# The down projection of a pair as seven block products, with its banks released earlier

## The chip, the cores and the metric

The kernel runs on one core of a Trainium2 chip. The metric is device time in microseconds, from launch to end of the program on that core. Five engines take part: PE (matmul; its weight loads are shown as PEld), DVE (elementwise and reductions, reads SBUF and PSUM), ACT (activation functions and scaled copies), POOL (elementwise on SBUF, gathers by index) and SP (issues most transfers). Each runs its own instructions in order and waits for others at semaphores.

## The reference, cut to what matters

One transformer block on 4096 tokens of width 256, in f32. Both branches start from the normalised input `xn`.

```python
xn = layernorm(x)
# attention, 8 heads of 32, window of 64: each token sees 64 before and 64 after
o   = softmax(q k3 * scale, masked to the band) v3
x1  = layernorm2(xn + o @ Wo + bo)
att = x1 + gelu(x1 @ W1 + b1) @ W2 + b2
# experts: 8 of them, the 2 best per token, hidden width 816
h   = silu((xn @ gw[e].T + gb[e]) * (xn @ uw[e].T + ub[e]))
ffn = sum over the two experts of weight * (h @ down_w[e].T + down_b[e])
return x + att + ffn
```

The change concerns `h @ down_w.T + down_b`, the down projection of the experts.

## The kernel before, in words

**Stages.** A first stage (to about 79 us) normalises, projects keys, queries and values for the first groups, and computes the routing: each token goes to two slots, sorted by expert. Slots are cut into *units* of one expert each: a *pair* is two tiles of 128 tokens, a *single* is one tile. 34 units always run: 30 pairs and, as units 3, 7, 11 and 15, four singles. Five more run only if the routing needs them. After the units comes the second feed-forward stage of the attention branch (from about 861 us), which already uses seven block products in place of eight for its second matmul (`second`, line 1189).

**The loop over units** (line 1259). The engine order is written out by hand: the order of the calls is the order on every engine. Units 0 to 31 also carry a piece of attention: unit b treats query tiles i and i+1 (i even) and one half of the heads (hq = b % 2). A unit does, in this order:

- `gather(b+2)`: POOL fetches token rows for a later unit (L819).
- `scores`: PE (L960) into four banks; DVE adds the mask and takes the maximum, eight times 128x256 (L974). `apart`: POOL, two differences of values into `xd` (L1009).
- `down_rest` for unit b-1: PE, the last 48 hidden rows (L896). They lie twice in the chunk `FCM` of the hidden tile, at partitions 0 and 64, one for each tile of a pair.
- three gate/up chunks (`chunk`, i.e. `glu`: PE L845, ACT L853, DVE L854) are mixed with eight exponentials on ACT (L989) and four `merge`s on POOL: each adds the two halves of a head's keys (L1001) and then multiplies the second half with the identity matrix to keep its diagonal (L1002). Only chunks 0 and 1 come before the scaling.
- in even units `closing`: the output projection of two tiles finished earlier (PE L1074), its residual and statistics on DVE (L1077), and `residual`: a load and a POOL sum (L1067).
- `scale`: DVE takes reciprocals (L1019), multiplies the first halves (L1021, needs all merges' sums), sums the diagonals (L1022, needs the last L1002), L1023; POOL scales `xd` (L1025).
- `down` for unit b-1: PE `results` (L907), 6 chunks x 1 or 2 tiles; DVE adds the bias out of the banks (`summed`, L917); SP stores `y`; then the next down weights are loaded.
- `turned(b+1)`: PE transposes the next unit's rows (L832), DVE copies (L837). Units below 16 (and 16) also project keys, values or queries for a later group; units 3, 7, 11 and 15 queries, copied by DVE (L286).
- chunk 2, `flip` 0 (PE L1030, DVE two masked copies L1034), chunk 3, `flip` 1, `flip_rest` (PE transposes `xd`, L1043; ACT L1045), chunk 4, `glu_rest` (L862, L866, L869), silu on ACT (L886), chunk 5, `weigh` (PE L1052, reads the flips' copies), `outputs` (DVE L1061).

**What sets the order around the change.** Seven PSUM banks (pool `psm`) rotate through nearly all these steps: a tile takes the bank that was released first in the order of the calls. `xd` and the probabilities `pr` have one buffer each, down weights `wd` two, hidden tiles `hTs` two (units b-1 and b).

Of the kernel before, what the change touches and what calls it, by code (L numbers as in the profile page):

```python
# [55 lines left out]


REM = FE % P
REM_UP = P // 2
FM = FE - REM  # L60
FCM = FM // P
NT = S // P
G = 512
# [27 lines left out]
GU = BW + 2 * FCM + 1  # L91
DN = FCE * D + D
HQ = 4
# [8 lines left out]
def block_kernel(ctx: ExitStack, tc: tile.TileContext, a: dict, out: bass.AP):  # L102
# [118 lines left out]
    wqkv = pool(att, "wqkv", right)  # L221
    mask = wqkv.tile([P, 4, 2 * P], F32, tag="mask", name="mask")

# [87 lines left out]
    def make_mask():  # L311

        nc.gpsimd.memset(mask, 0.0)
        for kind in range(4):

            def keep(base, step, channel, m=mask[:, kind, :]):
                nc.gpsimd.affine_select(
                    out=m,  # L320
                    in_=m,
                    compare_op=ALU.is_ge,
                    fill=MASKED,
                    base=base,
                    pattern=[[step, 2 * P]],
                    channel_multiplier=channel,
                )

            keep(0, 1, -1)
            keep(2 * WIN, -1, 1)  # L330
            if kind == 0:
                keep(-WIN, 1, 0)
            if kind == 3:
                keep(2 * P - WIN - 1, -1, 0)
        for m, base, step in ((first_keys, 0, 1), (second_keys, -1, -1)):
            nc.gpsimd.memset(m, 1.0)
            nc.gpsimd.affine_select(
                out=m,
                in_=m,
                compare_op=ALU.is_ge,  # L340
                fill=0.0,
                base=base,
                pattern=[[-step, P]],
                channel_multiplier=step,
            )
# [542 lines left out]
    def silu_rest(hT):  # L888

        silu(hT, FCM, FCE, slice(0, REM_UP + REM if hT.shape[2] > P else REM))  # L890

    def results_rest(pds, w, hT):
        for t, pd in enumerate(pds):

            half = slice(t * REM_UP, (t + 1) * REM_UP) if len(pds) > 1 else slice(0, P)
            nc.tensor.matmul(  # L896
                pd,
                hT[half, FCM, t * P : (t + 1) * P],
                w[half, FCM * D : FCE * D],
                start=True,  # L900
                stop=False,
            )
# [11 lines left out]

    def summed(y, pds, w):
        for t, pd in enumerate(pds):
            nc.vector.tensor_tensor(y[:, t, :], pd, w[:, FCE * D :], ALU.add)  # L917

# [5 lines left out]

    def down(b, pds, w, hT):
        at, n, _ = UNITS[b]
        results(pds, w, hT)
        y = he.tile([P, TB, D], F32, tag="y", name=f"y{b}")[:, 0:n, :]
        summed(y, pds, w)
        nc.sync.dma_start(out=rows(done, at, n), in_=y)  # L930

    def whole(b, w, wd, xT, hT, banks, gss, y):

        _, n, _ = UNITS[b]
        n_in = n * P
        for k, f in enumerate([FCM] + list(range(FCM))):
            pb = halves(banks[k % 3])[:, :, 0:n_in]
            gs = gss[k % 3][:, 0:n_in]
            if f == FCM:
                rest_of(w, xT, hT, pb, gs)  # L940
            else:
                chunk_of(f, w, xT, hT, pb, gs)
            if f == FCM:
                silu_rest(hT)
            elif f % 2:
                silu(hT, f - 1, f + 1)
        pds = [banks[k][:, 0:D] for k in (3, 1)[:n]]
        results_rest(pds, wd, hT)
        results(pds, wd, hT)
        summed(y, pds, wd)  # L950

    def scores(i, hq):
# [3 lines left out]
        for j in range(2):  # L956
            lo = (i + j) % TG * P
            for hh in range(HQ):
# [7 lines left out]
                )  # L966
        kind = 0 if i == 0 else 2 if i == NT - 2 else 1
        pr = sp.tile([P, HQ, 2, 2 * P], F32, tag="pr", name=f"pr{i}_{hq}", bufs=1)
# [3 lines left out]
        for hh in range(HQ):  # L972
            for j in range(2):
                nc.vector.tensor_tensor_reduce(  # L974
                    out=pr[:, hh, j, :],
                    in0=ps[hh][:, j, :],
                    in1=mask[:, kind + j, :],
                    scale=-1.0,
                    scalar=-LOWEST,
                    op0=ALU.add,  # L980
                    op1=ALU.min,
                    accum_out=nm[:, j, hh : hh + 1],
                )
# [29 lines left out]

    def scale(i, hq, pr, sums, xd):

        rec = sp.tile([P, 2, HQ], F32, tag="rec", name=f"rec{i}_{hq}")
        same = sp.tile([P, 2, HQ], F32, tag="same", name=f"same{i}_{hq}")
        by_head = "p j h -> p h j"
        nc.vector.reciprocal(rec, sums)  # L1019
        first = pr[:, :, :, 0:P]  # L1020
        nc.vector.tensor_tensor(first, first, bcast(rec.rearrange(by_head), P, 3), ALU.mult)  # L1021
        nc.vector.tensor_reduce(same.rearrange(by_head), pr[:, :, :, P:], AX.X, ALU.add)  # L1022
        nc.vector.tensor_tensor(same, same, rec, ALU.mult)  # L1023
        xh = xd.rearrange("p j (h d) -> p j h d", h=HQ)
        nc.gpsimd.tensor_tensor(xh, xh, bcast(same, DH, 3), ALU.mult)  # L1025

    def flip(i, hq, j, pr):
# [3 lines left out]

        prT = [sp.tile([P, HQ, P], F32, tag="prT", name=f"prT{i}_{hq}_{j}"), pr[:, :, j, P:]]
        for t, m in zip(prT, (first_keys, second_keys)):
# [209 lines left out]
    for k in range(2):  # L1243
        nc.gpsimd.memset(hTs[k][:, FCM, :], 0.0)
    res = {0: residual(0)}
    xT = {}
# [12 lines left out]
    for b in range(ALWAYS):  # L1259
# [5 lines left out]
        def chunk(f):  # L1265
            glu(b, f, gus[b], xT[b], hT)

        if b + 2 < ALWAYS:
            xs[b + 2] = gather(b + 2)
        if attends:  # L1270
            pr, nm, sums = scores(i, hq)
            xd = apart(i, hq)
        if 0 < b < STEPS:
            pds = down_rest(b - 1, downs[b - 1], hTs[(b - 1) % 2])
        if b == 0:
            xT[0] = turned(0, xs.pop(0))
        if attends:
            exps(pr, nm, sums, 0, 3)
            merge(pr, 0)
        chunk(0)  # L1280
        if b >= STEPS:
            pds = down_rest(b - 1, downs[b - 1], hTs[(b - 1) % 2])
            down(b - 1, pds, downs.pop(b - 1), hTs[(b - 1) % 2])
        if attends:
# [7 lines left out]
        if hq == 0 and i - 2 in res:  # L1292
            closing(i - 2, oTs.pop(i - 2), res.pop(i - 2))
            if i < STEPS:
                res[i] = residual(i)
        if attends:
            scale(i, hq, pr, sums, xd)
        if b == STEPS:
# [16 lines left out]
        if b == STEPS + 1:  # L1315
# [4 lines left out]
            x2s[0] = second_loads(0)  # L1320
        if 0 < b < STEPS:
            down(b - 1, pds, downs.pop(b - 1), hTs[(b - 1) % 2])
        if b == ALWAYS - 1:
# [30 lines left out]
        if attends:  # L1354
# [4 lines left out]
            prT1 = flip(i, hq, 1, pr)  # L1359
            added = flip_rest(i, hq, xd)  # L1360
        if b:
            chunk(4)
        n = b - (ALWAYS - len(MAYBE))
        if n >= 0:
# [18 lines left out]
    pds = down_rest(ALWAYS - 1, downs[ALWAYS - 1], last)  # L1383
    down(ALWAYS - 1, pds, downs.pop(ALWAYS - 1), last)
    load_unit(ALWAYS + 2)
# [141 lines left out]
```

## Time and profile before

| what | us |
|---|---|
| three runs: median (lowest to highest) | 1088.48 (1086.47 to 1089.20) |
| the profiled execution, its own time | 1084.23 |
| its span, first to last instruction | 1082.1 |
| units with attention (0 to 31), from their first scores to the start of unit 32 | about 79 to 777 |

The profile page gives busy time by engine and by line. The groups that the change touches (line, engine, operation; busy in us, mean in ns):

| group | count | busy | mean |
|---|---|---|---|
| L907 PE, down projection, 128x256 | 768 | 171.6 | 379 |
| L896 PE, its last rows, 64x256 | 120 | 21.1 | 428 |
| L917 DVE, bias out of the bank, 128x256 | 64 | 24.6 | 418 |
| L1021 DVE, scaling, 128x1024 | 32 | 39.5 | 1236 |
| L1022 DVE, diagonal sums, 128x1024 | 32 | 39.1 | 1221 |
| L1034 DVE, masked copies of the flips, 128x512 | 128 | 87.0 | 680 |
| L1001 POOL, merges, 128x256 | 128 | 93.0 | 727 |
| L1002 POOL, diagonals, 128x256 | 128 | 125.2 | 978 |

A matmul's mean is longer than its spacing, since matmuls overlap in the pipeline: for PE the distance from start to start is what counts. In a timeline, each line has the start, the duration, engine, line and operation, output<-inputs, shapes, how many instructions were merged into it, and in brackets the idle time before it with what ended it.

### The profile page before, as it was taken

How to read it: one execution, taken by the hardware profiler on the slowest of the kernel's cores; microseconds unless marked ns; L12 is line 12 of the kernel's file. 1: busy time of each engine (PE TensorE's matmuls, PEld its weight loads, DVE VectorE, ACT ScalarE, POOL GpSimd, SP SyncE). 2: the span in 40 equal slices, each digit the busy share in tenths (PEclk: the TensorE clock that was granted, in tenths of full speed). 3: DMA queues.
4: the chain of work that ended last, by engine and by line, in shares of the span. 5: the costliest groups of instructions: out<-in, count | busy, mean ns of one | idle time of the engine just before them, and what ended most of it. 6: DMA issues, size and time to landing. Idle time of an engine off the chain costs nothing. (4 is left out here: it accounts for less than half of the span.)

```text
span 1082.1 us, 19049 instructions
## 1 busy us (share of the span) xinstructions
PE 1068.8 (99%) x6802; PEld 857.1 (79%) x6802; DVE 657.5 (61%) x1709; ACT 526.7 (49%) x1225; POOL 451.6 (42%) x599
## 2 busy tenths in 40 slices
PE   9998999999999999999999999999999999999998
PEld 6577887887888788888888888888788847777778
DVE  6665766657666566666666766666533355555546
ACT  4526456654556546746564566455424363333320
POOL 5516544455445444554455535544520043322220
PEclk9999999999999999999999999999999999999999
DMA  8252445544445354545444545445666443333121
GB/s 282 76 215 97 142 140 179 178 144 154 159 143 192 125 174 149 201 142 175 159 175 142 197 142 189 142 161 169 191 213 228 158 146 105 101 98 97 59 64 40
DMA packets 61040, 163.42 MB, mean 151 GB/s; under 512 B 6576, under 2 KB 46896, under 8 KB 51472
## 3 DMA queue, kind: packets, MB, share of 16 engines
q1 hardware_dynamic: 53632, 144.18, 38.2%
q0 software_dynamic: 6480, 17.70, 6.1%
q8 instruction: 55, 0.90, 0.3%
q10 hardware_dynamic: 832, 0.30, 0.1%
q14 instruction: 41, 0.34, 0.1%
HBM read 140.28 MB, written 21.89 MB: 150 GB/s over the span
## 5 line engine op out<-in xcount | busy, mean ns | idle before, releaser
L845 PE MATMUL gu<-xsT,wg 128*128 128x256 f32 (+1 forms) x1632 | 363.1, 369 | 1.6 <-issue 1.5
L845 PEld LDWEIGHTS gu<-xsT,wg 128*128 128x128 f32 x1632 | 289.0, 190 | 46.9 <-DVE nm L974 8.6
L853 ACT ACTIVATE gs<-gu,wg 128x256 f32<-128x256 f32 (+1 forms) x204 | 92.4, 453 | 257.8 <-PE gu L845 254.8
L854 DVE SCALAR_TENSOR_TENSOR hT<-gu,wg,gs 128x256 f32<-128x256 f32 (+1 forms) x204 | 95.0, 467 | 177.0 <-ACT gs L853 173.6
L1001 POOL TENSOR_TENSOR pr<-pr 128x256 f32<-128x256 f32 x128 | 93.0, 727 | 247.9 <-ACT pr L989 247.9
L907 PE MATMUL pe<-wd,hT 128*128 128x256 f32 x768 | 171.6, 379 | 0.0
L907 PEld LDWEIGHTS pe<-wd,hT 128*128 128x128 f32 x768 | 145.4, 190 | 20.5 <-issue 1.0
L1172 POOL DMA_INDIRECT got<-done,slot x64 | 64.5, 1008 | 176.6 <-DVE acc L1185 109.4
L1002 POOL TENSOR_TENSOR pr<-pr,ident 128x256 f32<-128x256 f32 x128 | 125.2, 978 | 10.0
L989 ACT ACTIVATE pr<-pr,nm 128x256 f32<-128x256 f32 x256 | 126.8, 497 | 0.4
L1127 PE MATMUL ph<-x2T,W 128*128 128x512 f32 x256 | 111.4, 593 | 1.1 <-ACT x2T L1117 1.1
L974 DVE CUSTOM_DVE_ANT_0 pr<-ps,mask 128x256 f32<-128x256 f32 x256 | 90.7, 420 | 19.3 <-PE ps L960 19.3
L1134 ACT ACTIVATE hf<-ph,b 128x512 f32<-128x512 f32 x64 | 43.4, 688 | 116.5 <-PE ph L1127 57.9
L886 ACT ACTIVATE hT<-hT 128x512 f32<-128x512 f32 (+3 forms) x148 | 80.9, 546 | 32.0 <-DVE hT L854 21.8
L1127 PEld LDWEIGHTS ph<-x2T,W 128*128 128x128 f32 x256 | 48.0, 190 | 58.9 <-issue 52.9
L819 POOL DMA_INDIRECT xs<-xnd,token x71 | 68.8, 969 | 49.2 <-DVE paired_tiles L786 31.9
L1021 DVE TENSOR_TENSOR pr<-pr,rec 128x1024 f32<-128x1024 f32 x32 | 39.5, 1236 | 27.8 <-POOL pr L1001 27.8
L1208 DVE TENSOR_TENSOR acc<-u,acc 128x256 f32<-128x256 f32 x32 | 12.9, 423 | 70.9 <-ACT u L1211 70.3
L989 ACT ACT_TABLE_LOAD x31 | 39.8, 1283 | 23.8 <-DVE nm L974 23.7
L1022 DVE TENSOR_REDUCE same<-pr 128x8 f32<-128x1024 f32 x32 | 39.1, 1221 | 19.2 <-POOL pr L1002 19.2
L989 ACT ACTIVATION_READ_ACCUMULATOR pr<-pr,nm 128x1 f32 x256 | 48.5, 189 | 0.0
L1198 PE MATMUL s<-V,hv 128*128 128x128 f32 x384 | 44.2, 275 | 0.0
(231 smaller groups left out, 1572.0 us busy)
## 6 DMA issues: line engine op xcount, KB each, us to landing
wg<-in_gate_up SPq DMA_DIRECT2D x37, 1670.5 KB, 7.0
wd<-in_down SPq DMA_DIRECT2D x37, 1024.0 KB
done<-y SPq DMA_DIRECT2D x30, 256.0 KB
x<-in_x SPq DMA_DIRECT2D x8, 512.0 KB, 5.9
xnd<-xn SPq DMA_DIRECT2D x8, 512.0 KB
res<-xnd SPq DMA_DIRECT2D x16, 256.0 KB
x1d<-res SPq DMA_DIRECT2D x16, 256.0 KB
x<-x1d SPq DMA_DIRECT2D x8, 512.0 KB
```

The costliest lines, as they stand in the source:

```text
L819: nc.gpsimd.indirect_dma_start(out=x[:, t, :], out_offset=None, in_=xnd, in_offset=bass.IndirectOffsetOnAxis(ap=token[:, i : i + 1], axis=0),)
L845: nc.tensor.matmul(pb[:, k, :], w[:, lo : lo + P], xT[:, c, :], start=(c == 0), stop=(c == DC - 1),)
L853: nc.scalar.activation(gs, pb[:, 0, :], AF.Identity, bias=w[:, gb : gb + 1])
L854: nc.vector.scalar_tensor_tensor(hT[:, f, :], pb[:, 1, :], w[:, ub : ub + 1], gs, ALU.add, ALU.mult)
L886: nc.scalar.activation(hT[on, lo:hi, :], hT[on, lo:hi, :], AF.Silu)
L907: nc.tensor.matmul(pd, hT[:, f, t * P : (t + 1) * P], w[:, f * D : (f + 1) * D], start=False, stop=(f == FCM - 1),)
L974: nc.vector.tensor_tensor_reduce(out=pr[:, hh, j, :], in0=ps[hh][:, j, :], in1=mask[:, kind + j, :], scale=-1.0, scalar=-LOWEST, op0=ALU.a ...
L989: nc.scalar.activation(pr[:, hh, j, :], pr[:, hh, j, :], AF.Exp, bias=nm[:, j, hh : hh + 1], scale=-1.0, accum_out=sums[:, j, hh : hh + 1],)
L1001: nc.gpsimd.tensor_tensor(first, first, second, ALU.add)
L1002: nc.gpsimd.tensor_tensor(second, second, bcast(ident, 2, 1), ALU.mult)
L1127: nc.tensor.matmul(ph, W1[:, c, f * P : (f + 1) * P], x2T[:, c, :], start=(c == 0), stop=(c == DC - 1),)
L1172: nc.gpsimd.indirect_dma_start(out=y, out_offset=None, in_=done, in_offset=bass.IndirectOffsetOnAxis(ap=slot[:, k, i : i + 1], axis=0),)
```

## The change

For a pair whose down projection falls into units 1 to 31, the six full chunks are no longer 2 tiles x 6 chunks of 128x256. The hidden tile and the weights are cut into 2 x 2 blocks (two token tiles, even and odd chunks, two halves of the output columns), and the Winograd form of Strassen's scheme makes the result from seven products of blocks with 3 chunks of 128x128 each. It needs sums of blocks beforehand and afterwards:

- `sums_of_down`: four subtractions of weights on POOL, 128x384 each, behind `apart`; one overwrites a block of the weights.
- `sums_of_experts_hidden`: three sums of hidden blocks on DVE behind the scores, ahead of chunk 0; a fourth (line 970) stands on DVE between the first product and the last.
- `results_of_pair`: the products; three go into the two banks of the unit, four share one further bank `sh`.
- `summed_of_pair`: ACT copies the shared bank into `y`; DVE adds within `y`, then adds the two banks.

PE does these products where `down` stood, ahead of `turned`. On DVE the sums behind them stand between the scaling and the diagonal's sum: `scale` is cut in two, and `scale_rest` comes after. `flip_rest` moves from before chunk 4 to after it. The bias of the down projection becomes a row of the weights behind the last 48 rows; the hidden tiles carry ones in rows 48 and 112, set once by POOL after the first gathers. The weights lose their broadcast bias (1024 to 896 KB), and `summed` becomes a copy. Silu on the last rows runs on 48 rows for each tile, so that the ones stay. The flips' first copy is written in place into `pr`, and the mask has three kinds in place of four; both free room.

```diff
-        silu(hT, FCM, FCE, slice(0, REM_UP + REM if hT.shape[2] > P else REM))
+        for t in range(hT.shape[2] // P):
+            silu(hT[:, :, t * P : (t + 1) * P], FCM, FCE, slice(t * REM_UP, t * REM_UP + REM))
...
+    def sums_of_down(b, w):
+        ts = he.tile([P, 3, FCH, P], F32, tag="ts", name=f"ts{b}", bufs=1)
+        t2, t3, t4 = (ts[:, k] for k in range(3))
+        m = blocks_of_weights(w)
+        b11, b12, b21, b22 = m[:, 0, 0], m[:, 0, 1], m[:, 1, 0], m[:, 1, 1]
+        t1 = b12
+        for out_, left_, right_ in ((t3, b22, b12), (t1, b12, b11), (t2, b22, t1), (t4, b21, t2)):
+            nc.gpsimd.tensor_tensor(out_, left_, right_, ALU.subtract)
+        return ts
+
+    def sums_of_experts_hidden(b, hT):
+        ss = he.tile([P, 2, FCH, P], F32, tag="ss", name=f"ss{b}", bufs=1)
...
+        nc.vector.tensor_tensor(s1, a21, a22, ALU.add)
+        nc.vector.tensor_tensor(s2, s1, a11, ALU.subtract)
+        nc.vector.tensor_tensor(a21, a11, a21, ALU.subtract)
+        return ss
+
+    def results_of_pair(b, pds, w, hT, ss, ts):
...
+        shared = bank(f"sh{b}").rearrange("p (k n) -> p k n", n=P)
+        product(pds[0][:, c1], n[:, 0, 1], m[:, 1, 0], stop=False)
+        nc.vector.tensor_tensor(n[:, 0, 1], n[:, 0, 1], ss[:, 1], ALU.subtract)
+        product(pds[1][:, c1], n[:, 1, 1], ts[:, 2])
+        product(shared[:, 0], n[:, 0, 0], m[:, 0, 0], True)
+        product(shared[:, 1], ss[:, 1], ts[:, 0], True)
+        product(shared[:, 2], n[:, 1, 0], ts[:, 1], True)
+        product(shared[:, 3], ss[:, 0], m[:, 0, 1], True)
+        product(pds[0][:, c2], n[:, 0, 1], m[:, 1, 1])
+        return shared
+
+    def summed_of_pair(y, pds, shared):
+        q = y.rearrange("p t (h n) -> p (t h) n", n=P)
+        nc.scalar.copy(q, shared)
+        yield
+        nc.vector.tensor_tensor(q[:, 1], q[:, 0], q[:, 1], ALU.add)
+        nc.vector.tensor_tensor(q[:, 2], q[:, 1], q[:, 2], ALU.add)
+        both = q.rearrange("p (t h) n -> p h t n", h=2)
+        nc.vector.tensor_tensor(both[:, 1], q[:, 1:3], bcast(q[:, 3], 2, 1), ALU.add)
         for t, pd in enumerate(pds):
-            nc.vector.tensor_tensor(y[:, t, :], pd, w[:, FCE * D :], ALU.add)
+            nc.vector.tensor_tensor(y[:, t, :], pd, y[:, t, :], ALU.add)
...
-        prT = [sp.tile([P, HQ, P], F32, tag="prT", name=f"prT{i}_{hq}_{j}"), pr[:, :, j, P:]]
+        prT = [pr[:, :, j, k * P : (k + 1) * P] for k in range(2)]
...
     for k in range(2):
         nc.gpsimd.memset(hTs[k][:, FCM, :], 0.0)
+        for behind in (REM, REM_UP + REM):
+            nc.gpsimd.tensor_tensor(
+                hTs[k][:, FCM, :],
+                hTs[k][:, FCM, :],
+                ident[:, behind : behind + 1].to_broadcast([P, B]),
+                ALU.add,
+            )
...
         if attends:
             pr, nm, sums = scores(i, hq)
             xd = apart(i, hq)
+        ts = ss = None
+        if 0 < b < STEPS and UNITS[b - 1][1] > 1:
+            ts = sums_of_down(b - 1, downs[b - 1])
...
             merge(pr, 0)
+        if ts:
+            ss = sums_of_experts_hidden(b - 1, before)
         chunk(0)
...
+        made = iter(())
+        if 0 < b < STEPS:
+            made = down(b - 1, pds, downs.pop(b - 1), before, (ss, ts))
+            next(made)
         if attends:
-            scale(i, hq, pr, sums, xd)
+            rec = scale(i, hq, pr, sums)
+            list(made)
+            scale_rest(i, hq, pr, rec, xd)
...
-        if 0 < b < STEPS:
-            down(b - 1, pds, downs.pop(b - 1), hTs[(b - 1) % 2])
...
             prT1 = flip(i, hq, 1, pr)
-            added = flip_rest(i, hq, xd)
         if b:
             chunk(4)
+        if attends:
+            added = flip_rest(i, hq, xd)
```

## The prediction

> **What bounds the kernel now.** I read the busy shares, then the chain that ended last, then the timelines of PE, DVE and POOL in single units. Busy shares:
>
> ```profile
> PE 1068.8 (99%) x6802; PEld 857.1 (79%) x6802; DVE 657.5 (61%) x1709; ACT 526.7 (49%) x1225; POOL 451.6 (42%) x599
> ```
>
> PE streams all the time, and its listed waits add up to some 10 us. So time falls only if PE gets less work, and rises by whatever makes PE wait. For PE's pace, PE's timeline in unit 3, and one piece of the chain of waits (start, duration, what):
>
> ```profile
> 149.50 5.35 PE L907 MATMUL pe<-wd,hT 128*128 128x256 f32 x24
> 154.69 0.60 PE L832 MATMUL pts<-ident,xs 128*128 128x128 f32 x4
> ```
>
> ```profile
> 891.64 12.51 PE s L1198 x112
> ```
>
> Start to start, 24 matmul records of 256 columns take 154.69 - 149.50 = 5.19 us, 0.216 each. The second stage already runs block products of 128 columns: 12.51 / 112 = 0.112 each. (A product of f32 tiles shows as two records.)
>
> Behind PE the other engines have uneven slack. The reader should look at unit 3 (one tile after a pair), DVE and PE:
>
> ```profile
> 155.27 1.22 DVE L1021 TENSOR_TENSOR pr<-pr,rec 128x1024 f32<-128x1024 f32 x1 [1.62 <-POOL pr L1001]
> 157.12 1.22 DVE L1022 TENSOR_REDUCE same<-pr 128x8 f32<-128x1024 f32 x1 [0.62 <-POOL pr L1002]
> 158.37 0.17 DVE L1023 TENSOR_TENSOR same<-same,rec 128x8 f32<-128x8 f32 x1
> 158.48 0.76 DVE L917 TENSOR_TENSOR y<-pe,wd 128x256 f32<-128x256 f32 x2
> 159.15 0.68 DVE L837 COPY xsT<-pts 128x512 f32<-128x512 f32 x1
> 159.75 1.40 DVE L286 TENSOR_SCALAR qt<-q,bq 128x512 f32<-128x512 f32 x2
> ...
> 163.38 0.68 DVE L1034 TENSOR_TENSOR pr<-pT,second_keys 128x512 f32<-128x512 f32 x1
> ...
> 164.22 0.40 PE L1052 MATMUL po<-prT,vt 128*32 128x128 f32 x8
> ```
>
> From L1022 on DVE has no gap, and its last masked copy ends at 163.38 + 0.68 = 164.06; PE reads it at 164.22. **Margin 0.16 us**: here DVE is as late as PE. Units 7, 11 and 15 show the same (252.82 against 252.99, 341.59 against 341.75, 430.35 against 430.51). The chain starts on POOL: the scaling L1021 waits for the fourth merge (L1001).
>
> **The change part by part.**
>
> *PE.* Units 1 to 31 without 4, 8, 12, 16 (whose predecessor is one tile) do the down projection of a pair: 27. Each had 24 records, 5.19 us; now 7 products x 3 chunks x 2 records = 42 at 0.112 = 4.69. Gain 0.50 each. Here a rule speaks against the change: the Trainium skill (TensorE: Matmul & The Clock Gate, Back-to-back issue gap) says that spacing in a stream of loads and matmuls is set by both, sustained 81 ns at N=128 against 131 at N=512. By that flat curve (linear between, 256 columns would be near 98) halving the columns would save 17%: 42 x 0.179 = 7.5 us, a loss of 2.3 per pair, 63 in all. But the trace has the very shape, f32 with a fresh load for each, at 0.112; I take the row. Upper bound by the 16 narrow records of unit 3 from 147.62 to 149.50: 0.1175 each, gain 0.25.
>
> *DVE before the scaling.* Three sums of 128x384, placed behind the scores and ahead of the first gate product, and a fourth inside the products. No row has 384; between 128x256 (0.42, L1208) and 128x1024 (1.22, L1159) it is 0.56. DVE's own gaps there (0.83 and 1.37 us in unit 3) hide three; the fourth needs DVE while PE runs five products of 0.67, so PE rarely waits for it (in unit 3, at worst 0.6, inside time that DVE sets anyway). What they do to POOL is not hidden. Two moments:
>
> ```profile
> 155.32 1.76 POOL L1002 TENSOR_TENSOR pr<-pr,ident 128x256 f32<-128x256 f32 x1
> ```
>
> ```profile
> 131.46 1.58 DVE L1021 TENSOR_TENSOR pr<-pr,rec 128x1024 f32<-128x1024 f32 x1 [0.47 <-POOL pr L1001]
> 131.23 0.73 POOL L1002 TENSOR_TENSOR pr<-pr,ident 128x256 f32<-128x256 f32 x1
> ```
>
> A POOL sum (0.73 alone) that starts under DVE's scaling takes 1.76: 1.03 lost to a DVE op of 1.22. In the one case where POOL was first, POOL kept 0.73 and DVE took 1.58 instead of 1.22. The Trainium skill (SBUF — State Buffer, Who interferes with whom) has it as a lock: a DVE instruction with two SBUF inputs shares a read interface with GpSimd, and whoever is first holds it for the whole instruction. The whole instruction would be 4 x 0.56 = 2.2 us on the merges; by the row (op less 0.19) it is 4 x 0.37 = 1.5. The merges run back to back from 150.04, just as the scores end, so there is no gap to take it. Least: 0.4, if most sums fall between POOL's instructions. I take 1.5.
>
> *DVE behind the scaling.* `summed_of_pair` adds two sums of 128x128 and one of 128x256, each dependent on the last: 0.29 (between 0.17 at 8 elements and 0.42) twice, 0.42, 0.1 between them: 1.1 us. The two adds out of the banks cost what L917 costs, only earlier. The 0.62 that L1022 waited for POOL's last merge goes into it; that merge now meets these sums: 0 to 0.5, say 0.25. The flips no longer write a tile of their own, same cost.
>
> *The chain in units 3, 7, 11, 15:* 1.5 + 1.1 - 0.62 + 0.25 = 2.2, less the margin 0.16: **2.1 us each, 8.4 in all** (0.7 to 2.6). There DVE sets the end, so PE's 0.50 does not show: 23 x 0.50 = 11.6 is left.
>
> *Odd units 17 to 31* (8, without projections for later groups):
>
> ```profile
> 678.31 1.23 DVE L1021 TENSOR_TENSOR pr<-pr,rec 128x1024 f32<-128x1024 f32 x1 [1.41 <-POOL pr L1001]
> 681.55 0.60 PE L1030 MATMUL pT<-ident,pr 128*128 128x128 f32 x4
> ```
>
> The flips need the scaling, done at 679.54: slack 2.0. PE comes 0.5 earlier, the scaling 1.5 later: none is left. Lateness carried from the even unit before then stalls PE one to one. If DVE has caught up (even units have 1.7 us more PE work, `closing`): 0. If POOL's residual sum (L1067, 1.27) gets in between the new DVE sums of an even unit: up to 1.6. I take 0.75 each, 6.0. Odd units below 16 with a pair have 1.7 us or more of projections on PE: nothing.
>
> *Start.* Four POOL sums of 128x256 put ones behind the hidden rows: 4 x 0.7 (0.73 in L1001, 0.62 in L1025) = 2.8, behind the first gathers and ahead of everything of unit 0:
>
> ```profile
> 84.42 0.46 POOL L1009 TENSOR_TENSOR xd<-vt 128x128 f32<-128x128 f32 x1
> 85.45 0.73 POOL L1001 TENSOR_TENSOR pr<-pr 128x256 f32<-128x256 f32 x1 [0.56 <-ACT pr L989]
> 92.53 0.65 PE L1030 MATMUL pT<-ident,pr 128*128 128x128 f32 x4 [0.48 <-DVE pr L1021]
> ```
>
> POOL waits here 0.56 and, at the second head, 0.53; the rest, 1.7, goes into the merges and on to the flips, for which PE waits already. 1.7 (1.2 to 2.2).
>
> *At nothing.* POOL's sums of down weights, 4 x 1.0 (between 0.73 at 256 and 1.27 at 512 elements), stand behind `apart` and two gathers; POOL idles 8.38 us before the first merge (L1001 in units 3, 7, 11, 15; similar elsewhere), of which the later scaling takes some 2.2: 2 us stay. With that gone they would delay merges, scaling and flips one to one. Their weights land a unit earlier, and with 896 instead of 1024 KB. ACT: the bank copy 0.59 in its gap of 5.15 us before the third gate product; two small silu instead of one, +0.2. Bias as a matmul row instead of an add: L917 becomes a copy out of PSUM, 0.42 either way. The transposes of `xd` go behind the fifth gate chunk, so L1009 starts 2 us later, in the same idle time. Banks: the order of instructions gives those of the down projection to the second flip and later; both are free by then. SP's queue keeps its order; the store of y comes earlier.
>
> **Sum:** -11.6 + 8.4 + 6.0 + 1.7 = +4.5 us. The profiled execution's own time is 1084.23 (span 1082.1), below all three runs shown; changed runs are measured like those, so I set the sum on their median: 1088.5 + 4.5 = **1093.0**.
>
> **The rivals.**
> *Port costs little* (faster): the chain takes 0.4 for the four sums and nothing for the last merge, so 0.4 + 1.1 - 0.62 - 0.16 = 0.7 in four units, odd units stall 0, start 1.2: -11.6 + 2.9 + 1.2 = -7.5, 1081. For it: DVE has 39% free and its gaps cover the sums. Against: both rows of the port above.
> *Balance* (no change): chain 2.0, odd units 0.25: -11.6 + 8.0 + 2.0 + 1.7 = +0.1, 1088.6. Decided by whether even units let DVE catch up.
> *POOL gets in everywhere:* 2.6 in four units, 1.6 in eight, start 2.2: -11.6 + 10.4 + 12.8 + 2.2 = +13.8, 1102.
> *Narrow products don't keep their pace* (the change doesn't do what it says): gain 0.25, 5.8 in all: +10.3, 1098.8. Against: 112 records at 0.112.
>
> **How the numbers follow.** Forecast 0.36, port costs little 0.28, balance 0.18, POOL everywhere 0.12, pace lost 0.06. This kernel's runs tell about 0.3% from no change, 3.3 us. Faster 0.28, same 0.18, slower 0.54. The range takes in the faster rival and most of the worst: 1080 to 1101; the forecast's own is 1090 to 1097.
>
> **What would show it.** Right: the block products at 4.7 us a pair; the scaling 1.5 us later behind the scores; POOL merges of 1.1 us under DVE's sums; in units 3, 7, 11, 15 PE waiting at `weigh` for DVE some 2 us; PE waits at the flips in odd units from 17. Wrong: merges still at 0.73 and no PE waits at `weigh` (faster), or waits inside the products for the fourth sum.

## The result and the profile after

| | median | lowest to highest | runs |
|---|---|---|---|
| before | 1086.83 us | 1086.44 to 1089.20 | 5 |
| after | 1081.93 us | 1081.21 to 1083.35 | 5 |

The ratio of after to before is 0.9951, with a 95% interval of 0.9938 to 0.9964: the change makes the kernel 0.5% **faster**. I had forecast 1093.0 us, slower. The kernel before was run again beside the experiments below, 35 runs in three groups with medians of 1087.44, 1087.12 and 1087.75.

The busy shares of the profiled execution of the changed kernel (1082.42 us, span 1080.7):

```profile
PE 1063.6 (98%) x7288; PEld 861.0 (80%) x7288; DVE 779.3 (72%) x1898; ACT 547.8 (51%) x1283; POOL 588.0 (54%) x709
```

DVE is busy 122 us longer and POOL 136 us, PE 5 us less. The kernel got faster all the same, because most of the new work lies in time that DVE and POOL had free. The table shows where it does not. A unit's length is the distance from the start of its first scores on PE's timeline to that of the next unit's:

| units | before | after | difference, us |
|---|---|---|---|
| 0 | 19.81 | 21.40 | +1.59 |
| 1, 2, 5, 6, 9, 10, 13, 14 and 17 to 31: pair behind a pair (23) | 20.85 to 24.09 | 20.36 to 23.61 | -0.49 each |
| 3, 7, 11, 15: single behind a pair | 18.86 | 20.43 | +1.57 each |
| 4, 8, 12 (pair behind a single) | 23.23 | 23.42 | +0.19 each |
| 16 (pair behind a single) | 20.69 | 20.88 | +0.19 |

From the first scores to the start of unit 31 (the length of unit 31 itself can't be read this way) these sum to 1.6 - 22 x 0.49 + 4 x 1.57 + 4 x 0.19 = -2.1 us; the traces show 676.39 before and 674.30 after. From there to the end this one execution took 326.89 us against 326.29 before, and six of the kernels below, with nearly the same work there, 325.8 to 326.4: the 0.6 us are not read as an effect of the change.

**The gain** is read in unit 23, PE's timeline after the change (start, duration, line):

```profile
589.21 0.83 PE L960 MATMUL pe<-wd,hT 128*128 128x128 f32 x6
589.88 0.83 PE L960 MATMUL pe<-ts,hT 128*128 128x128 f32 x6
...
593.90 0.60 PE L834 MATMUL pts<-ident,xs 128*128 128x128 f32 x4
594.33 1.89 PE L847 MATMUL gu<-xsT,wg 128*128 128x256 f32 x8
596.06 0.60 PE L1118 MATMUL pT<-ident,pr 128*128 128x128 f32 x4
```

Seven products take 593.90 - 589.21 = 4.69 us, 0.67 each and without a wait between them; and the flip (L1118) follows its neighbour without a bracket, so PE doesn't wait there for the scaling. In the kernel before, DVE's scaling and PE's flip of this unit stood so:

```profile
591.44 1.22 DVE L1021 TENSOR_TENSOR pr<-pr,rec 128x1024 f32<-128x1024 f32 x1 [1.41 <-POOL pr L1001]
594.67 0.60 PE L1030 MATMUL pT<-ident,pr 128*128 128x128 f32 x4
```

The scaling was done 2.0 us before the flip; after the change (L1100 below) 596.06 - 595.57 = 0.5 us are left.

**The cost** on DVE and POOL in the same unit; the sums of the hidden layer are L946, L947, L948 and L970, the merges L1082 and L1083:

```profile
587.87 0.55 DVE L946 TENSOR_TENSOR ss<-hT 128x384 f32<-128x384 f32 x1
588.46 0.97 DVE L947 TENSOR_TENSOR ss<-ss,hT 128x384 f32<-128x384 f32 x1
589.35 1.08 DVE L948 TENSOR_TENSOR hT<-hT 128x384 f32<-128x384 f32 x1
...
591.13 1.10 DVE L970 TENSOR_TENSOR hT<-hT,ss 128x384 f32<-128x384 f32 x1
...
594.34 1.23 DVE L1100 TENSOR_TENSOR pr<-pr,rec 128x1024 f32<-128x1024 f32 x1 [2.00 <-POOL pr L1082]
595.49 0.82 DVE L983 TENSOR_TENSOR y<-y 128x128 f32<-128x128 f32 x1
596.34 0.29 DVE L984 TENSOR_TENSOR y<-y 128x128 f32<-128x128 f32 x1
```

```profile
588.08 0.93 POOL L1082 TENSOR_TENSOR pr<-pr 128x256 f32<-128x256 f32 x1 [1.43 <-ACT pr L1070]
589.09 0.92 POOL L1083 TENSOR_TENSOR pr<-pr,ident 128x256 f32<-128x256 f32 x1
589.97 1.04 POOL L1082 TENSOR_TENSOR pr<-pr 128x256 f32<-128x256 f32 x1
...
593.58 0.73 POOL L1082 TENSOR_TENSOR pr<-pr 128x256 f32<-128x256 f32 x1
594.39 1.77 POOL L1083 TENSOR_TENSOR pr<-pr,ident 128x256 f32<-128x256 f32 x1
```

Alone a sum takes 0.55 and a merge 0.73. Where they overlap, both become longer, in turns: a merge waits for the sum that runs (0.93), the next sum for the merge (0.97), and so on. The sums lose more by it (0.4 to 0.55 each) than the merges (0.2 to 0.3). So the scaling L1100 starts 10.4 us after the first scores, against 9.4 before, 1.0 later. Behind it the last diagonal (L1083, 1.77) and the first sum of the results (L983, 0.82 instead of 0.29) meet in the same way.

**Where it can't be hidden**: unit 3, DVE, and then PE.

```profile
160.39 1.21 DVE L1108 TENSOR_REDUCE same<-pr 128x8 f32<-128x1024 f32 x1
...
161.72 0.68 DVE L839 COPY xsT<-pts 128x512 f32<-128x512 f32 x1
162.32 1.40 DVE L288 TENSOR_SCALAR qt<-q,bq 128x512 f32<-128x512 f32 x2
...
165.94 0.68 DVE L1122 TENSOR_TENSOR pr<-pT,second_keys 128x512 f32<-128x512 f32 x1
```

```profile
162.45 1.16 PE L847 MATMUL gu<-xsT,wg 128*128 128x128 f32 x8 [0.51 <-DVE xsT L839]
...
166.68 0.43 PE L1140 MATMUL po<-pr,vt 128*32 128x128 f32 x8 [0.17 <-DVE pr L1122]
```

DVE works without a gap from the scaling to the last masked copy, which ends at 165.94 + 0.68 = 166.62, and PE's last group of `weigh` starts just behind it. PE waits twice for this chain, and the unit is 1.57 us longer.

### The profile page after: what moved, and what is told of

The parts are those of the page before. It is cut to its first block, busy times and chain, and to the rows that moved or that the text cites. A ratio compares the mean times of both kernels' runs of the same rounds, so it can differ in the third digit from the quotient of the medians.

```text
span 1080.7 us, 20405 instructions
## 1 busy us (share of the span) xinstructions
PE 1063.6 (98%) x7288; PEld 861.0 (80%) x7288; DVE 779.3 (72%) x1898; ACT 547.8 (51%) x1283; POOL 588.0 (54%) x709
## 5 line engine op out<-in xcount | busy, mean ns | idle before, releaser
L1082 POOL TENSOR_TENSOR pr<-pr 128x256 f32<-128x256 f32 x128 | 114.1, 891 | 73.0 <-ACT pr L1070 73.0
L856 DVE SCALAR_TENSOR_TENSOR hT<-gu,wg,gs 128x256 f32<-128x256 f32 (+1 forms) x204 | 91.6, 460 | 65.7 <-ACT gs L855 64.3
L1083 POOL TENSOR_TENSOR pr<-pr,ident 128x256 f32<-128x256 f32 x128 | 132.5, 1035 | 10.0
L888 ACT ACTIVATE hT<-hT 128x512 f32<-128x512 f32 (+2 forms) x179 | 85.8, 486 | 49.6 <-DVE hT L856 25.2
L1055 DVE CUSTOM_DVE_ANT_0 pr<-ps,mask 128x256 f32<-128x256 f32 x256 | 90.7, 420 | 10.4 <-PE ps L1041 10.3
L1100 DVE TENSOR_TENSOR pr<-pr,rec 128x1024 f32<-128x1024 f32 x32 | 39.2, 1225 | 42.3 <-POOL pr L1082 42.3
L1113 POOL TENSOR_TENSOR xd<-xd,same 128x256 f32<-128x256 f32 x32 | 19.7, 615 | 84.7 <-DVE same L1111 84.6
L937 POOL TENSOR_TENSOR ts<-wd 128x384 f32<-128x384 f32 x54 | 54.1, 1002 | 2.1
L981 ACT COPY y<-sh 128x512 f32<-128x512 f32 x27 | 15.8, 585 | 58.9 <-PE sh L960 58.9
L960 PE MATMUL pe<-wd,hT 128*128 128x128 f32 x324 | 44.9, 275 | 0.0
```

The costliest lines, as they stand in the source:

```text
L856: nc.vector.scalar_tensor_tensor(hT[:, f, :], pb[:, 1, :], w[:, ub : ub + 1], gs, ALU.add, ALU.mult)
L888: nc.scalar.activation(hT[on, lo:hi, :], hT[on, lo:hi, :], AF.Silu)
L1055: nc.vector.tensor_tensor_reduce(out=pr[:, hh, j, :], in0=ps[hh][:, j, :], in1=mask[:, kinds[j], :], scale=-1.0, scalar=-LOWEST, op0=ALU.a ...
L1082: nc.gpsimd.tensor_tensor(first, first, second, ALU.add)
L1083: nc.gpsimd.tensor_tensor(second, second, bcast(ident, 2, 1), ALU.mult)
```

## The experiments

Each starts from the changed kernel and makes one edit, where nothing else is said. Times are to be compared with its 1081.93 us; ratios are to the kernel before. "Theory 1" and "theory 2" are those of the expectation just above.

### The block products are left out

```diff
-        if 0 < b < STEPS and UNITS[b - 1][1] > 1:
+        if 0 < b < 1 and UNITS[b - 1][1] > 1:
             ts = sums_of_down(b - 1, downs[b - 1])
```

> All pairs' down products are computed in full, nothing else is changed (the bias as a row of the rest, the later small transposes, the masked copies in place and the sums behind scaling stay). Theory 1: the block products are what the time came from, 0.49 us in each of 23 pair units less 1.77 us around each of four single units: without them 1081.9 + 11.3 - 7.1 = about 1086.1 us (ratio 0.9995 to the kernel before), with the first unit still 1.6 us longer and units 17 to 31 at 20.85 us. Theory 2: the shorter units come from the small edits (bias row, smaller weights' load, later transposes): 1075 to 1082 us (0.989 to 0.995).

Measured: 1088.58 us, ratio 1.0016 (1.0007 to 1.0025). The units are as theory 1 had it: 20.86 us in the odd ones from 17 (+0.49), 18.86 in units 3, 7, 11 and 15, the first still 21.39; 4, 8, 12 and 16 stay at 23.42 and 20.88. By its units the products are worth 23 x 0.49 - 4 x 1.57 = 5.0 us; the medians lie 6.65 apart, and where the rest comes from the traces don't show. The remaining edits alone make the kernel no faster, rather 1 us slower by the medians, and 2.3 by the units (1.58 in the first, 0.19 in each of four). The gain comes from the products.

### No block products in the four single units

```diff
-        if 0 < b < STEPS and UNITS[b - 1][1] > 1:
+        if 0 < b < STEPS and UNITS[b - 1][1] > 1 and UNITS[b][1] > 1:
```

> The block products are kept where the unit over them attends to a pair itself; in units 3, 7, 11 and 15 (a single block over a pair's down products) the pair's down is computed in full as before. Theory 1: in these four units the chain of VectorE (scaling, sums of the products, diagonal, queries, masked copies) sets the end, and the port lost 1.57 us in each and 0.20 us in the unit after it: units 3, 7, 11, 15 go back from 20.43 to 18.86 us between their scores, and the kernel to 1081.9 - 4 x 1.77 = about 1075 us (ratio to the kernel before 0.989). Theory 2: TensorE sets the end there too, and the four units lose the 0.49 us that the block products save: about 1084 us (0.997).

Measured: 1075.81 us, ratio 0.9893 (0.9879 to 0.9908). Units 3, 7, 11 and 15 take 18.87 us, and PE waits nowhere in them. Theory 1 holds for these four: there the chain of DVE takes more than the products give. Its other half falls: units 4, 8, 12 and 16 keep their 23.42 and 20.88, so their 0.19 us is not lateness carried over from the single unit.

### Without the sums of the hidden layer

```diff
-        nc.vector.tensor_tensor(s1, a21, a22, ALU.add)
-        nc.vector.tensor_tensor(s2, s1, a11, ALU.subtract)
-        nc.vector.tensor_tensor(a21, a11, a21, ALU.subtract)
-        return ss
+        return ss0
...
-        nc.vector.tensor_tensor(n[:, 0, 1], n[:, 0, 1], ss[:, 1], ALU.subtract)
```

> VectorE's four sums of the hidden layer are left out (the block products read a tile of zeros for the two sums and the two blocks unchanged), so the results of pairs in the attention units are not the reference's; all products and the sums behind them stay. Theory 1: these sums, taking turns with GpSimd's merges, cost the single units 0.9 us ahead of scaling and 0.5 us at the first sum behind it: merges at 0.73 us, scaling 8.3 instead of 9.2 to 9.3 us after the scores, units 3, 7, 11, 15 at 18.9 to 19.1 instead of 20.43 us, the kernel at 1081.9 - 4 x 1.4 - 4 x 0.2 = about 1075.5 us (0.989). Theory 2: what lengthens these units is the five sums behind the scaling, not the ones ahead of it: units 3, 7, 11, 15 stay above 20 us, and the kernel at about 1081 (0.9945).

Measured: 1078.56 us, ratio 0.9918 (0.9905 to 0.9931). Units 3, 7, 11 and 15 take 19.55 us, between the two theories: of the 1.57 us, 0.88 came from the sums ahead of the scaling. POOL and DVE in unit 3 of this kernel, whose line numbers are 8 lower in these places:

```profile
151.96 0.73 POOL L1074 TENSOR_TENSOR pr<-pr 128x256 f32<-128x256 f32 x1 [2.46 <-ACT pr L1062]
...
157.24 1.76 POOL L1075 TENSOR_TENSOR pr<-pr,ident 128x256 f32<-128x256 f32 x1
```

```profile
157.20 1.22 DVE L1092 TENSOR_TENSOR pr<-pr,rec 128x1024 f32<-128x1024 f32 x1 [1.62 <-POOL pr L1074]
158.34 0.81 DVE L975 TENSOR_TENSOR y<-y 128x128 f32<-128x128 f32 x1
```

The merges are back at 0.73, so it was the sums that had stretched them. But the first sum behind the scaling (L975) still takes 0.81: it meets POOL's last diagonal whenever that one starts together with the scaling, and costs 0.52 whether or not there were sums before. My theory 1 had put that down to the lateness.

### The queries evacuated by ACT in the four single units

```diff
-                    queries(ahead, c, False)
+                    queries(ahead, c, UNITS[b][1] < 2)
```

> In units 3, 7, 11 and 15 the two evacuations of the queries (0.67 us each) move from VectorE to ScalarE, nothing else. Theory 1: in these four units one gapless chain on VectorE, from the scaling to the second masked copy, sets the end; it becomes 1.3 us shorter, so the units go from 20.43 to about 19.1 us and the kernel to 1081.9 - 4 x 1.3 = about 1076.7 us (ratio 0.990). Theory 2: the wait is for GpSimd's merges or for a bank: the units stay at 20.4 us and the kernel at 1082 (0.995).

Measured: 1077.38 us, ratio 0.9913 (0.9896 to 0.9929); the four units take 19.13 us, 1.30 less. PE in unit 3 of this kernel:

```profile
164.40 0.88 PE L1140 MATMUL po<-pr,vt 128*32 128x128 f32 x24
165.45 0.43 PE L1140 MATMUL po<-pr,vt 128*32 128x128 f32 x8 [0.17 <-DVE pr L1122]
```

Work of 1.3 us taken off DVE shortens the unit by 1.3 us: DVE sets the end, and even now the last masked copy is what PE waits for. Theory 1 holds.

### The small transposes go back

```diff
             prT1 = flip(i, hq, 1, pr)
+            added = flip_rest(i, hq, xd)
         if b:
             chunk(4)
-        if attends:
-            added = flip_rest(i, hq, xd)
```

> Only the small transposes go back ahead of the fifth chunk, where they were before the change. Theory 1: that they come 1.7 us later is what keeps units 17 to 31 free of a stall: the small values are scaled 1.3 us after TensorE gets to them, so each of the eight odd units 17 to 31 becomes 1.3 us longer (20.37 to about 21.6 us) and the kernel about 1081.9 + 8 x 1.3 = 1092 us (ratio 1.004); the units with keys or values between are unchanged. Theory 2: the move is free either way, TensorE waits nowhere else more: 1082 us (0.995).

Measured: 1097.31 us, ratio 1.0096 (1.0080 to 1.0111). Theory 1 holds with its mechanism, and the place is larger than it said. PE in unit 23 of this kernel:

```profile
605.82 0.60 PE L1118 MATMUL pT<-ident,pr 128*128 128x128 f32 x4
607.62 0.44 PE L1131 MATMUL pX<-ident,xd 128*128 128x128 f32 x2 [1.20 <-POOL xd L1113]
```

The odd units 17 to 29 take 1.41 us more and the even ones 18 to 28 another 0.62 to 0.75, 13.8 us to the start of unit 31. The sums that DVE now does ahead of the diagonal's make the scaled `xd` late, and only the later place of its transposes hides it.

In this profile the first unit is 1.5 us longer as well, but the edit leaves that unit's order as it was. PE's clock fell there. The two flips of the first unit in this kernel, a row of its stretches (us, each engine's busy time, PEclk the granted clock, DMA share, GB/s), and the two flips in the next kernel, where the clock stayed at 1.00:

```profile
94.00 0.66 PE L1118 MATMUL pT<-ident,pr 128*128 128x128 f32 x4 [2.84 <-DVE pr L1100]
97.27 1.06 PE L1118 MATMUL pT<-ident,pr 128*128 128x128 f32 x4
```

```profile
96.00:97.00 1.00, 1.00 (x4) 0.82 (x3) 1.00 (x3) 0.00 (x0) 0.79 (x2) 0.50 0.00 0
```

```profile
94.11 0.66 PE L1118 MATMUL pT<-ident,pr 128*128 128x128 f32 x4 [2.73 <-DVE pr L1100]
96.33 0.60 PE L1118 MATMUL pT<-ident,pr 128*128 128x128 f32 x4
```

From flip to flip PE takes 3.27 us instead of 2.22, and the rest is lost right behind. So a fall of the clock behind the wait for the scaling costs the unit its full 1.5 us.

### The sums go behind the diagonal

```diff
             rec = scale(i, hq, pr, sums)
-            list(made)
             scale_rest(i, hq, pr, rec, xd)
+            list(made)
```

> Only the order on VectorE behind the scaling: the diagonal's reduction and its product first, then the sums of the down products, as before the change. Theory 1: the seven banks are not short, nothing waits for those of the products, and VectorE's chain keeps its length: every unit as before within 0.1 us, the kernel at 1081.5 to 1082.5 us. Theory 2: the banks of the products, freed 1.4 us later, are what the next transposes or chunks need: 0.3 to 1.4 us more in most of the 27 units with products, the kernel at 1090 us or more (above 1.002).

Measured: 1093.34 us, ratio 1.0062 (1.0046 to 1.0077). Theory 2 has the mechanism, with its place narrower: 0.93 us in each odd unit from 17, 0.50 in the single ones, 0.25 in unit 1, nothing in the rest, 8.8 us to the start of unit 31. A row of the table of waits on PE, and its place in unit 23:

```profile
PE gu L847 <- DVE y L989: 10.3, 11, 1.4
```

```profile
603.21 0.60 PE L1118 MATMUL pT<-ident,pr 128*128 128x128 f32 x4
604.48 1.99 PE L847 MATMUL gu<-xsT,wg 128*128 128x256 f32 x8 [0.67 <-DVE y L989]
```

(The row has the waits' sum, their number and the longest.) The fifth gate chunk takes a bank that L989, the add of the results, has to read first. In unit 23 after the change the two adds of L989 start 13.25 us after the scores, and the chunk 14.73; with the sums behind the diagonal L989 starts at 15.07, 1.8 us later, and PE stands still.

### Fillers that keep TensorE busy in the first unit

```diff
         if b == 0:
+            idle = bank("idle0")
+            for n in range(10):
+                nc.tensor.transpose(idle[:, 0:P], ident, ident)
             xT[0] = turned(0, xs.pop(0))
+            for n in range(6):
+                nc.tensor.transpose(idle[:, P : 2 * P], ident, ident)
```

> Sixteen transposes of the identity are added where TensorE idles in the first unit: ten between the scores and the transposes of the tokens, six behind these. Theory 1: the first unit takes 21.4 us instead of the 19.8 of the kernel before's profile because TensorE idles there for 2.3 of 3.2 us and its clock is granted at half for the next 3.5 us; without the idling the clock stays at 1.00 at 84 to 88 us, the first chunks take 3.6 instead of 5.2 us, the first unit 19.8 to 20.0, the kernel 1.6 us less, about 1080.3 us. Theory 2: the clock falls for another reason (the load before): then the first unit stays at 21.4 us or more and the kernel at 1081.9 to 1082.5.

Measured: 1081.84 us, ratio 0.9953 (0.9939 to 0.9966). The first unit stays at 21.39 us, as in theory 2, but not for its reason. Stretches after the change and with the fillers (us, each engine's busy time, PEclk the granted clock, DMA share, GB/s):

```profile
84.00:85.00 1.00, 1.00 (x3) 0.82 (x4) 0.00 (x0) 1.00 (x5) 0.85 (x2) 0.50 0.00 0
86.00:87.00 1.00, 1.00 (x4) 0.78 (x3) 0.00 (x0) 0.00 (x0) 0.99 (x2) 0.50 0.44 131
```

```profile
84.00:85.00 1.00, 0.94 (x8) 0.70 (x7) 0.00 (x0) 0.82 (x2) 0.85 (x2) 1.00 0.00 0
86.00:87.00 1.00, 1.00 (x6) 0.90 (x5) 0.00 (x0) 0.34 (x3) 0.98 (x2) 1.00 0.43 131
```

The clock stays at 1.00 and the first chunks take 3.6 instead of 5.2 us; then PE waits longer for the scaling, 1.78 instead of 1.06 us, and its flip starts at the same time, since POOL's merges, late by the rows of ones, still set the scaling:

```profile
94.21 0.63 PE L1118 MATMUL pT<-ident,pr 128*128 128x128 f32 x4 [1.78 <-DVE pr L1100]
```

### The rows of ones earlier

```diff
-    xs = {b: gather(b) for b in range(2)}
-
     hTs = [he.tile([P, FCE, B], F32, tag=f"hT{k}", name=f"hT{k}", bufs=1) for k in range(2)]
     for k in range(2):
         nc.gpsimd.memset(hTs[k][:, FCM, :], 0.0)
...
+
+    xs = {b: gather(b) for b in range(2)}
     res = {0: residual(0)}
```

> The hidden layer's two tiles are cleared and given their rows of ones before the first gathers, where GpSimd idles, not behind them. Theory 1: the four additions of about 0.65 us stand ahead of the first merges and so made the first unit later: the merges start at 85.5 instead of 87.7 us after the span's start, TensorE's wait at the first flip falls from 1.06 to about 0.5 us, and the kernel takes 1.6 us less, about 1080.3 (ratio 0.994). Theory 2: the first unit was longer because TensorE's clock was granted at half at 84 to 87.5 us in the profile after the change (first chunks 5.24 instead of 3.55 us): then the merges come early but the first unit stays at 21.2 to 21.4 us and the kernel at 1081.9 (0.995).

Measured: 1081.20 us, ratio 0.9944 (0.9932 to 0.9956). In its profile the first unit takes 21.62 us: the clock is at 0.50 from before 84 to some 90 us, longer than in the changed kernel's profile, and hides what the earlier merges bring.

### Both together

The edits of the last two runs.

> The filler transposes of one run and the early rows of ones of another together. Theory 1: the first unit has two causes of the same size that hide each other, TensorE's halved clock and GpSimd's late merges: with both gone the first flip waits 0.5 instead of 1.1 to 1.8 us and the first unit takes 19.8 to 20.1 us, the kernel 1081.9 - 1.4 = about 1080.5 us (ratio 0.994). Theory 2: something else is late there (the tokens' gathers): the first unit stays at 21.4 us, the kernel at 1081.9 us.

Measured: 1081.24 us, ratio 0.9940 (0.9926 to 0.9954); the first unit takes 20.20 us.

```profile
93.53 0.63 PE L1118 MATMUL pT<-ident,pr 128*128 128x128 f32 x4 [0.62 <-DVE pr L1100]
```

So the two causes are there, and each hides the other: one taken away gains nothing in the first unit, both gain 1.2 us. In the kernel's time it is 0.7 us of medians whose runs spread by 2, which by itself would show nothing.

### All rows in the rest of single units

```diff
-            half = slice(t * REM_UP, (t + 1) * REM_UP)
+            half = slice(t * REM_UP, (t + 1) * REM_UP) if len(pds) > 1 else slice(0, P)
...
-        for behind in (REM, REM_UP + REM):
+        for t, behind in enumerate((REM, REM_UP + REM)):
+            ones = hTs[k][:, FCM, t * P : (t + 1) * P]
             nc.gpsimd.tensor_tensor(
-                hTs[k][:, FCM, :],
-                hTs[k][:, FCM, :],
-                ident[:, behind : behind + 1].to_broadcast([P, B]),
-                ALU.add,
+                ones, ones, ident[:, behind : behind + 1].to_broadcast([P, P]), ALU.add
             )
```

> For units of one block, the rest of the down product again reads all 128 rows, as before the change; so that the bias comes in once, each block's columns get ones in one row only. Theory 1: the product over 64 rows alone, between products over 128, is what made units 4, 8, 12 and 16 0.19 us longer (its 0.63 instead of 0.53 us, and 0.1 us more at the chunk behind it): they go from 23.42 and 20.88 back to 23.23 and 20.69 us, the kernel to 1081.9 - 0.8 = 1081.1 us. Theory 2: these units are longer because of the sums and copies that VectorE takes over: they stay, and the kernel is at 1081.9 us.

Measured: 1080.51 us, ratio 0.9932 (0.9917 to 0.9947). Units 4, 8, 12 and 16 take 23.23 and 20.69 us again. PE in unit 4, after the change and in this run:

```profile
168.11 0.70 PE L897 MATMUL pe<-wd,hT 64*128 64x256 f32 x2
168.73 3.72 PE L847 MATMUL gu<-xsT,wg 128*128 128x256 f32 x16
172.29 1.89 PE L1162 MATMUL wo<-Wo,oT 128*128 128x256 f32 x8
```

```profile
168.07 0.70 PE L897 MATMUL pe<-wd,hT 128*128 128x256 f32 x2
168.61 3.62 PE L847 MATMUL gu<-xsT,wg 128*128 128x256 f32 x16
172.06 1.89 PE L1162 MATMUL wo<-Wo,oT 128*128 128x256 f32 x8
```

Half the rows take 0.08 us longer start to start (0.62 against 0.54), and the chunk behind them 0.11 longer (3.56 against 3.45). Theory 1 holds. The first unit is shorter here too (20.76 us), with POOL adding the ones, half as wide, in 0.75 instead of 1.30 us a tile; that this is the cause is argued.

### Two versions that beat both kernels

The first has the edits of four runs: no products in single units, all rows, early ones, fillers.

> Four edits together: no block products in units 3, 7, 11 and 15, all rows in the rest of single units, early rows of ones, filler transposes. By the sum of the single runs: 1075.8 - 0.8 - 1.4 = 1073.6 us (ratio to the kernel before 0.9875); units 3, 7, 11, 15 at 18.87, 4, 8 and 12 at 23.23, 16 at 20.69, the first at 19.8 to 20.1 us. If edits cover the same time, 1075 us.

Measured: 1073.48 us, ratio 0.9870 (0.9854 to 0.9885), 0.8% less than the change. Its units are those expected (18.87, 23.23, 20.69, the first 20.15): the edits add up. The second keeps the products in the single units and moves DVE's copies there to ACT, the queries' as in the run above and those of the next unit's rows; rows, ones and fillers are those of the first:

```diff
-        copy = nc.vector.tensor_copy if b else nc.scalar.copy
+        copy = nc.vector.tensor_copy
+        if b == 0 or (b <= NT and UNITS[b - 1][1] < 2):
+            copy = nc.scalar.copy
```

> The block products stay in units 3, 7, 11 and 15, and there the queries' evacuations and the copy of the next unit's turned tokens (0.68 us) move from VectorE to ScalarE; with all rows in the rest of single units, early ones and filler transposes. Theory 1: VectorE's chain sets the end of these units and is 2.0 us shorter, so TensorE's own work sets it, 18.87 - 0.49 = 18.4 us: the kernel at 1081.9 - 4 x 2.0 - 0.8 - 1.4 = about 1071.7 us (0.986). Theory 2: ScalarE, loaded with three more evacuations, releases the chunks or the turned tokens later: units of 18.9 to 19.5 us, the kernel at 1074 to 1076 us.

Measured: 1073.72 us, ratio 0.9870 (0.9855 to 0.9885). The single units take 18.73 to 18.89 us, hardly less than without products, though PE no longer waits for the chain behind the scaling. PE in unit 3 of this kernel, and DVE's third sum there:

```profile
151.25 0.86 PE L962 MATMUL sh<-ts,ss 128*128 128x128 f32 x6
152.18 0.94 PE L962 MATMUL sh<-ts,hT 128*128 128x128 f32 x6
152.95 0.83 PE L962 MATMUL sh<-wd,ss 128*128 128x128 f32 x6
```

```profile
151.04 1.08 DVE L950 TENSOR_TENSOR hT<-hT 128x384 f32<-128x384 f32 x1
```

The fourth and fifth product take 0.93 and 0.77 us to the next instead of 0.67: behind a single tile's short first chunks (half the columns) PE gets to the fifth while DVE is still at its sum, which ends at 152.12. Without the sums of the hidden layer all seven take 0.67 there. That takes 0.36 of the 0.49 us, and units 4, 8 and 12 are at 23.28 to 23.43, for which no cause was looked for. Theory 1's path is gone, its gain isn't there; theory 2 had a small gain too, but put the loss on ACT.

## Why the prediction was wrong

I had summed +4.5 us. The changed kernel's median is 2.3 us below the profiled execution of before (1084.23). Term by term, against that execution:

| step | predicted | measured |
|---|---|---|
| PE, 23 pairs | -11.6 | -11.3 (0.49 each) |
| single units 3, 7, 11, 15 | +8.4 | +6.3 (1.57 each) |
| odd units 17 to 31 | +6.0 | 0 |
| start | +1.7 | +1.6 |
| single's rest on half the rows | not in the sum | +0.8 |
| sum | +4.5 | -2.6 |

**The step that failed is "Odd units 17 to 31 ... I take 0.75 each, 6.0".** Its balance was nearly right: PE 0.5 earlier, the scaling 1.0 later (I had 1.5), of 2.0 us of slack 0.5 is left, and the flip of unit 23 follows without a wait. What I added to it, lateness carried from the even unit, isn't there: DVE starts its first mask of unit 23 at 1.17 us after the first scores before and after the change, and each odd unit read is 0.49 shorter, as on PE alone. With no slack to spare and no row for a wait I had set a middle between 0 and 1.6 eight times; the row that speaks was my own, that even units have 1.7 us more work on PE to catch up in. The decision between my forecast and "balance" was named rightly: whether even units let DVE catch up. They do. (PE's -11.6 is 23 x 0.50 = 11.5.)

**The chain in single units** had the right place and mechanism, and the sum was 0.5 too large in each. Port: 1.5 predicted; 0.9 by the scaling's start (10.27 us after the first scores against 9.36), and 0.88 by the run without the sums. I had charged a sum's whole length but 0.19 to the merges. The Trainium skill (SBUF — State Buffer, Who interferes with whom) calls the port that DVE and POOL share an exclusive lock, and says of DVE's two-port modes that whoever issues first holds it for the whole instruction; what the rows show is that the two engines take turns, so that each waits for a part of the other's instruction, and that the sums pay more of it than the merges. Behind the scaling: 1.1 - 0.62 + 0.25 = 0.73 predicted, 0.96 measured (from the scaling's start to the end of the last copy 9.75 us against 8.79), since the first sum loses 0.52 to POOL's last diagonal. Margin: 0.16 predicted, from the third group of `weigh`; the wait that sets the end is the fourth group's, which in the kernel before started 164.44 - 164.06 = 0.38 after the copy's end:

```profile
164.44 0.40 PE L1052 MATMUL po<-pr,vt 128*32 128x128 f32 x8
```

By these, 0.91 + 0.96 - 0.38 = 1.5, against 1.57.

**What I had put at nothing** cost nothing in the changed kernel, but only together: the transposes' new place is worth some 14 us and the early release of the banks 9 (by the units, to the start of unit 31), by the two runs that undo them. "Both are free by then" was true by about 1 us for the fifth chunk. Not costed was that single units read half the rows of the rest, 0.19 us in each unit behind one.

**The start** has the size predicted against that execution. But there PE's clock stayed at 1.00, while in seven of ten profiles of kernels without fillers it fell to 0.50 at about 84 to 88 us; in the changed kernel POOL's late merges hide that. I had set the sum on the median, 1088.5, taking the changed kernel to be measured like the one before. But the 35 runs of before lie 1.1 to 5.5 us above its profiled execution, and the lower their mean granted clock, the longer they are: 1085.4 us on average at 1.000 (two runs), 1086.9 at 0.998 (15), 1088.0 at 0.996 and 0.997 (16), 1089.6 at 0.995 (two). The changed kernel's four runs at 0.998 average 1082.1. So of the 4.9 us between the medians, 2.3 are the distance from that execution, which the traces account for (2.6 by the table), and 2.6 are that execution's distance from its own median. That a fallen clock makes part of these, which the changed kernel would not pay again in its first unit, is argued: one fall cost 1.5 us where nothing hid it ("The small transposes go back"), but the other runs of before have no trace, and even those at 1.000 are over 1 us above the profiled one. It stays open.

The rival "port costs little" came to the right time by luck (-7.5 on the median, 1081; the units give -2.6): it was right that odd units don't stall, but its start was too low and its chain, 0.7 against 1.57, far too low, and the median that it stood on made up for them. The range (1080 to 1101) holds the time. The rule on the spacing of narrow products was rightly set aside: 0.67 us for six records, 0.112 each.

## What to carry to other kernels

Work added to engines that are half idle is free in most of a loop and costs most of its length where one of them already sets the end: sort the iterations by what ends them, price each kind apart, and leave the new work out where it doesn't pay (here four units of 32 gave 6 us back). Don't price an unseen wait with a middle value times a count; compute the slack, and if the lag has work to catch up in, take zero. When one profiled execution is the base, see how it stands to its own runs before setting the sum on their median.

## What was not expected of the hardware

- DVE's and POOL's sums at the same time stretch each other: a DVE sum of 128x384 takes 0.55 us alone and 0.97 to 1.10 beside POOL's merges (after the change, unit 23), a merge 0.73 alone and 0.92 to 1.05 beside the sums.
- After the change, PE's clock was granted at half for some 3.4 us although its longest idle stretch before was only 1.3 us, among pieces that made 2.3 of 3.2 us idle; in all four profiles with fillers it stayed at 1.00 there. Without them it stayed up there in three profiles of ten, one of which has the fall some 10 us later, so fillers are not its only condition. The Trainium skill (TensorE: Matmul & The Clock Gate, Part 1: The HAM clock gate) speaks of one idle window of about 3.4 us.
- A matmul over 64 of 128 rows between matmuls over 128 took 0.19 us more than one over all rows (units 4, 8, 12 and 16), 0.11 of it in the chunk behind.
